# Handing out on-chip buffers by the engine that read them last, and two reorderings, in a four-layer WKV and graph-convolution kernel

## The chip, the cores and the metric

The kernel runs on one core of a Trainium2 chip. Its time is the device time of one launch in microseconds (us), the median over runs. Five engines matter, and each works through its own list of instructions in order. PE (TensorE) multiplies matrices. DVE (VectorE) does the recurrences, the weighted sums and the products. ACT (ScalarE) does exponentials, logarithms and squares. POOL (GpSimd) does further elementwise work, and SP (SyncE) issues the DMA transfers. An instruction waits on a semaphore when another engine must have finished first. While it waits, everything behind it on its own engine waits too.

## The reference

The input `x` is 16 x 192 x 56 x 56 in float32, so there are 16 samples with 192 channels and 3136 positions each. Four layers follow one another, each as `x = x + layer(group_norm(x))`. Three layers are bidirectional WKV layers, and the fourth is a graph convolution with a batch norm and a GELU. Cut to what matters:

```python
def wkv_layer(x):                            # x is already group-normed
    xs = x.reshape(B, C, T).transpose(0, 2, 1)
    k, v, r = xs @ Wk.T, xs @ Wv.T, xs @ Wr.T
    x_bi = 0.5 * (wkv_scan(k, v) + flip(wkv_scan(flip(k), flip(v))))
    h = sigmoid(r) * x_bi
    h = layer_norm(h) * ln_g + ln_b          # over the channels
    return h @ Wo.T

# wkv_scan keeps two decayed sums along the positions:
#   p = decay * p + exp(k) * v,   q = decay * q + exp(k)
#   y = (p_before + exp(u + k) * v) / (q_before + exp(u + k))

def graph_layer(x):                          # x is already group-normed
    m = max(roll(x, 2, H) - x, roll(x, -2, H) - x, roll(x, 2, W) - x, roll(x, -2, W) - x, 0)
    return gelu(batch_norm(conv1x1(concat(x, m))))
```

## The kernel before

**Tiling.** Two samples are worked on together as a pair, which gives eight pairs. The 2 x 192 channels fill three blocks of 128 partitions. The positions are cut into seven chunks of `L = 448`. One tile holds one chunk of a pair: 128 partitions x 3 blocks x 448 positions, and a few columns at the edges for the carry of a scan. Such a tile is a *slot*; there are 33 (`NSLOTS`), and nearly all large data of the kernel lives in them: a chunk of `x`, the keys `ek = exp(k)`, the values `ekv = exp(k) * v`, the two scans' outputs `q` and `p`, the gate `sg`, and scratch for the graph layer. `class Slot` takes the slot that has been free for longest from the list `free`, and `give` puts one back at its end. A slot is given back in program order, when its last reader has been written into the program; whoever takes it next waits on a semaphore until that reader has really finished.

**Steps.** Two pairs are under way at a time, half a layer apart. Of one, the forward part is worked on (the functions `a_...`: keys, values, the scans `q` and `p` from left to right, and `y = p / q`). Of the other it is the backward part (`b_...`: the scans from right to left, the mix of both directions with the gate, the layer norm, the output product and its addition to `x`). One step does one chunk of each. The order of all instructions within a step is written out by hand in one function for each kind of step, and the program keeps that order on every engine. Mapped onto the trace, there are 85 steps `both_a`, 17 `both_a_first` (the first chunk of a layer's forward part), 42 `both_c` (a backward chunk beside a chunk of the graph layer), 66 `forward_a`, and 39 others.

**The functions that the change touches.** `scan` (line 870) takes a slot for its output and issues three scans on DVE, one for each block. `bonus` (line 885) issues two DVE instructions, one over two blocks and one over one; `a_den`, `a_num`, `b_den` and `b_num` call it. `a_p` is the forward scan `p`, followed by `save` (line 881), which copies its last column into the edge of the next chunk's `ekv`. `a_y` (line 977) is one POOL product over the whole tile. `b_mix` (lines 1026 to 1028) is nine POOL products and sums; at its end it gives back the slot of `ekv`, called `y` there, and that of `sg`. `b_sums` (lines 1042 and 1044) has PE add up squares for the layer norm. `b_rs1`, `b_rs2`, `b_rs3` (1050, 1058, 1060) make its deviation on ACT. `b_spread` (1066) spreads it over partitions on PE into `rsb`, `b_scale` (1071) multiplies by it on DVE, `b_out` is the output product on PE into `ops`, and `b_x` (1084) adds that to `x` on DVE. Of the group norm of a pair's next layer, `norm_var` (744 to 760) makes the variance on DVE from PE's result `psg` and two ACT instructions `rstd` (752, 753). `norm_fold` (772 to 775) refines it on DVE and folds it into the weights on ACT. The parts of these norms stand in one list, and each call of `gap()` takes the next part off it and issues it there. `c_rows` (1109 to 1111) and `c_columns` (1120 to 1124) are the neighbour maxima of the graph layer on DVE, and `c_product` its matrix product on PE.

Of the kernel before, what the change touches and what calls it, by code (L numbers as in the profile page):

```python
# [58 lines left out]
NSLOTS = 33  # L59
# [414 lines left out]
def fast_path(ctx: ExitStack, tc: tile.TileContext, flag, x, wproj, wfold, wcfold, wconst, wgroup, sums, picks, vecs, out):  # L474
# [22 lines left out]
        return f"{s}_{ngen[0]}"  # L497


    free = [f"slot{i}" for i in range(NSLOTS)]  # L500

    class Slot:
        def __init__(self, what):
            self.tag = free.pop(0)
            rows = keep.tile([P, 3, L + 4], F32, tag=self.tag, name=name(what))
            self.full, self.lead = rows[:, :, 2 : L + 3], rows[:, :, 1 : L + 2]
            self.t = rows[:, :, 2 : L + 2]

        def give(self):
            free.append(self.tag)  # L510


    free_banks = [f"bank{i}" for i in range(7)]
# [303 lines left out]
    def gap(eng=V):  # L817
        if norms:
            part, run = norms.pop(0)
            if part is norm_fold:  # L820
                part(run, eng)
            else:
                part(run)
# [35 lines left out]
    def scan(run, key, data, step, first):  # L859

        dec = params[run.l][0]
        s = Slot(key)
        for j in ORDER:
            if first:
                out, e = s.t[:, j, ::step], data.t[:, j, ::step]
            elif step > 0:
                out, e = s.lead[:, j, :], data.lead[:, j, :]
            else:
                out, e = s.full[:, j, ::-1], data.full[:, j, ::-1]
            V.tensor_tensor_scan(  # L870
                out, dec[:, column(j)].to_broadcast([P, L if first else L + 1]), e, 0.0, ALU.mult, ALU.add
            )
        return s

    def save(s, step, to, eng=G):

        src, dst = (s.t[:, :, L - 1 : L], to.lead[:, :, 0:1]) if step > 0 else (s.t[:, :, 0:1], to.full[:, :, L : L + 1])
        if eng is S:
            S.activation(dst, src, AF.Copy)  # L879
        else:  # L880
            eng.tensor_copy(dst, src)  # L881
# [5 lines left out]

    AHEAD, BACK = 1, -1

    def slot_of(slots, c, what):  # L890
        if c not in slots:
            slots[c] = Slot(what)
        return slots[c]


# [6 lines left out]
    def a_keys(run, c):  # L902
        if not once(run, "k", c):
            return
        product(run, "k", run.w[0], run.xa[c], c == 0)
        slot_of(run.ek, c, "ek")
        if c == 0:
            take_bias(run, "k", S)

# [41 lines left out]
    def a_p(run, c, eng=G):  # L951
        run.h[c] = scan(run, "p", run.ekv[c], AHEAD, c == 0)
        if c < NL - 1:
            save(run.h[c], AHEAD, slot_of(run.ekv, c + 1, "ekv"), eng)

    def a_den(run, c):
        if c in (0, NL - 1):
# [8 lines left out]
    def a_num(run, c):  # L966
        bonus(run, run.h[c], run.ekv[c], run.h[c])

    def ln(s, js=slice(0, 3)):
        S.activation(s.t[:, js, :], s.t[:, js, :], AF.Ln)  # L970

    def exp_minus(s, js=slice(0, 3)):
        S.activation(s.t[:, js, :], s.t[:, js, :], AF.Exp, scale=-1.0)  # L973

    def a_y(run, c):
        den = run.den.pop(c)
        G.tensor_mul(run.h[c].t, run.h[c].t, den.t)  # L977
        den.give()


    def b_gate(run, c):
# [25 lines left out]
    def b_den(run, c):  # L1007
        q = run.q.pop(c)
        bonus(run, run.ek[c], run.ek[c], q)
        q.give()  # L1010

    def b_p(run, c):
        if c not in run.p:
# [4 lines left out]
    def b_num(run, c):  # L1018
        p = run.p.pop(c)
        bonus(run, run.ekv[c], run.ekv[c], p)  # L1020
        p.give()

    def b_mix(run, c):
        y, h, sg, den = run.ekv.pop(c), run.h[c], run.sg.pop(c), run.ek[c]
        for j in ORDER:
            G.tensor_mul(y.t[:, j, :], y.t[:, j, :], den.t[:, j, :])  # L1026
            G.tensor_add(h.t[:, j, :], h.t[:, j, :], y.t[:, j, :])  # L1027
            G.tensor_mul(h.t[:, j, :], h.t[:, j, :], sg.t[:, j, :])  # L1028
        y.give()
        sg.give()  # L1030

    def b_squares(run, c, js=ORDER):
        h, sq = run.h[c].t, run.ek[c].t
# [3 lines left out]
    def b_sums(run, c):  # L1037
        h, sq = run.h[c].t, run.ek.pop(c)
        st = run.ps["st"] = bank("st")
        parts = ((h, 0), (h, 1), (sq.t, 0), (sq.t, 1))  # L1040
        for n, (t, i) in enumerate(parts):
            PE.matmul(st[32 * n : 32 * n + 32, :L], ones[:, 0, :], t[:, 2 * i, :], start=True, stop=False)
        for n, (t, i) in enumerate(parts):
            PE.matmul(st[32 * n : 32 * n + 32, :L], ones[:, 1 + i, :], t[:, 1, :], start=False, stop=n < 2)  # L1044
        sq.give()

    def b_rs1(run, c):
        rs, st = row.tile([P, L], F32, tag="rs", name=name("rs")), run.ps["st"]
# [25 lines left out]
    def b_out(run, c):  # L1074
        h = run.h.pop(c)
        run.ps["o"] = banks("ops")
        project(run.ps["o"], params[run.l][5], of(h.t), L)
        h.give()

    def b_x(run, c):  # L1080
        wob, ps, xs = params[run.l][4], run.ps["o"], run.xb[c]
# [31 lines left out]
    def c_columns(run, c):  # L1113

        m, xt, ml = run.m[c].t, run.xa[c].t, Slot("ml")
        run.ml[c] = ml
        for j in ORDER:
            xr = xt[:, j, :].rearrange("p (r w) -> p r w", w=W)
            mr = ml.t[:, j, :].rearrange("p (r w) -> p r w", w=W)
            V.tensor_max(mr[:, :, 2 : W - 2], xr[:, :, 0 : W - 4], xr[:, :, 4:W])  # L1120
            V.tensor_max(mr[:, :, 0:2], xr[:, :, W - 2 : W], xr[:, :, 2:4])
            V.tensor_max(mr[:, :, W - 2 : W], xr[:, :, W - 4 : W - 2], xr[:, :, 0:2])
        V.tensor_max(ml.t, ml.t, xt)  # L1123
        V.tensor_max(m, m, ml.t)
# [185 lines left out]
    def invert(t):  # L1310
        ln(t)
        exp_minus(t)
# [61 lines left out]
    def both_a_first(b, a, nback, nfront, loads):  # L1374

        den = lambda: a[0].den[a[1]]
        l = of_stage(0)
        load_ahead(nback)
        store()
        a_values(*a)  # L1380
        b_squares(*l, (0, 2))
        b_q(*b)
        b_sigmoid(*b)
        b_p(*b)
        b_den(*b)
        invert(b[0].ek[b[1]])
        b_num(*b)
        b_mix(*b)
        slot_of(a[0].ekv, a[1] + 1, "ekv")
        for u in loads:  # L1390
            load_ahead(u)
        a_ekv(*a)
        b_squares(*l, (1,))
        if nback is not None:
            b_gate(*nback[1:])
        b_sums(*l)
        b_rs1(*l)
        if nback is not None:
            b_exp(*nback[1:])
        a_q(*a)  # L1400
        b_rs2(*l)
        b_rs3(*l)
        keys(nfront)
        a_p(*a, V)
        spread_and_scale(l)
        b_squares(*b, (0,))
        a_save(*a)
        exp_keys(nfront)
        b_squares(*b, (2, 1))
        b_sums(*b)  # L1410
        a_den(*a)
        b_rs1(*b)
        ln(den())
        add(l)
        a_num(*a)
        late[b] = 0.5
        exp_minus(den())
        a_y(*a)

    def both_c(b, a, nback, nfront, loads):  # L1420

        l0, l1, l2 = of_stage(0), of_stage(1), of_stage(2)
        load_ahead(nback)
        first = nback is not None and not l1
        b_q(*b)
        b_p(*b)
        if first:

            b_gate(*nback[1:])
            b_exp(*nback[1:])  # L1430
            c_product(*a, 0)
        if l0:
            squares_and_sums(l0)
        b_den(*b)
        ln(b[0].ek[b[1]])
        if l0:
            b_rs1(*l0)
        exp_minus(b[0].ek[b[1]])
        if l2:
            add(l2)  # L1440
            sum_up()
        if l1:
            spread_and_scale(l1)
        gap()
        store()
        for u in loads:
            load_ahead(u)
        if nback is not None:
            if not first:
                b_gate(*nback[1:])  # L1450
                b_exp(*nback[1:])
        else:
            keys(nfront)
            exp_keys(nfront)
        if not first:
            c_product(*a, 0)
        c_rows(*a)
        if l0:
            b_rs2(*l0)
            b_rs3(*l0)  # L1460
            late[l0] = 1
        c_columns(*a)
        c_product(*a, 1)
        gap()
        gap()
        b_num(*b)
        b_sigmoid(*b)
        b_mix(*b)
        if l1:
            add(l1)  # L1470
            sum_up()
        if nback is not None:
            b_q(*nback[1:])
            b_p(*nback[1:])
        ahead = nback is None and l0 and nfront is not None and nfront[0] == "A"
        if ahead:
            a_q(*nfront[1:])
            a_save(*nfront[1:])
            b_spread(*l0)
            c_end(*a, False)  # L1480
            a_values(*nfront[1:])
            b_scale(*l0)
            b_out(*l0)
            late[l0] = 2
        elif l0:
            spread_and_scale(l0)
        if not ahead:
            c_end(*a, False)
        late[b] = 0
# [350 lines left out]
```

## Time and profile before

| what | value |
|---|---|
| median of 3 runs | 5248.44 us (5244.23 to 5249.13) |
| the profiled execution's own time | 5246.37 us |
| its span | 5244.4 us |
| DVE busy | 4837.0 us (92%), 6288 instructions |
| PE busy | 4701.2 us (90%), 15542 instructions |
| ACT busy | 3680.4 us (70%), 7163 instructions |
| POOL busy | 2900.0 us (55%), 2234 instructions |
| mean granted TensorE clock | 0.943 |
| DMA | 482.47 MB, mean 92 GB/s |

The profiled execution lies 2.1 us below the median. Its span is 2.0 us less than its own time, which is what lies around the program. "Busy" is time in which an engine had an instruction under way. The rest of an engine's span is idle, and the trace says which instruction of which engine ended each idle stretch. In the lines that follow, `p<-fdecays,ekv` is an instruction's output and its inputs by their names in the program, and `L870` is its line in the kernel. The number after the bar in a group's line is its busy time, then the mean of one instruction in ns, then the idle time just before these instructions with what ended most of it.

### The profile page before, as it was taken

Reading aid. Unit: us, or ns where it says so; the run is one execution under the profiler, and the core shown is the slowest. Engines: PE = TensorE matmul, PEld = TensorE weight load, DVE = VectorE, ACT = ScalarE, POOL = GpSimd, SP = SyncE. Lnnn points to the kernel's source line nnn. Section 1 sums busy time; section 2 is a strip of 40 time slices with the busy share of each in tenths; the row PEclk is TensorE's granted clock in tenths of the full one; section 3 lists DMA queues with packets and bytes.
Section 4 is the critical chain, followed back from the end, with each engine's and each line's share of the span. In section 5 each row is a group of like instructions: output and inputs, shape, how many; then the busy total and the mean of one; then the engine's idle time right before and its main releaser. Section 6 shows DMA issues by size and latency. Waiting matters only on the chain. (4 is left out here: it accounts for less than half of the span.)

```text
span 5244.4 us, 51899 instructions
## 1 busy us (share of the span) xinstructions
PE 4701.2 (90%) x15542; PEld 1493.0 (28%) x15542; DVE 4837.0 (92%) x6288; ACT 3680.4 (70%) x7163; POOL 2900.0 (55%) x2234
## 2 busy tenths in 40 slices
PE   7999998989899998898989999889898999999887
PEld 3222222223232222222323222222232322222222
DVE  6999889899999998999999999889999999999996
ACT  6777777776566777776656678778766667777672
POOL 1666555555455655555454556556545455666562
PEclk9999999999999999999999999999999999999998
DMA  5222222223232222223323223222332322222233
GB/s 153 69 82 82 95 82 92 85 90 116 89 116 71 87 90 88 85 85 100 118 79 113 84 74 100 87 78 93 115 100 87 111 74 76 75 83 81 73 108 114
DMA packets 314275, 482.47 MB, mean 92 GB/s; under 512 B 66432, under 2 KB 306688, under 8 KB 313984
## 3 DMA queue, kind: packets, MB, share of 16 engines
q1 hardware_dynamic: 312832, 477.59, 28.5%
q8 instruction: 125, 2.05, 0.2%
q10 hardware_dynamic: 1152, 1.48, 0.1%
q14 instruction: 166, 1.36, 0.1%
HBM read 324.83 MB, written 154.14 MB: 91 GB/s over the span
## 5 line engine op out<-in xcount | busy, mean ns | idle before, releaser
L870 DVE TENSOR_TENSOR_SCAN p<-fdecays,ekv 128x449 f32<-128x449 f32 (+1 forms) x1008 | 1021.9, 1069 | 113.8 <-POOL p L1027 60.1
L870 DVE TENSOR_TENSOR_SCAN q<-fdecays,ek 128x449 f32<-128x449 f32 (+1 forms) x1008 | 1024.7, 1072 | 8.9 <-ACT ek L915 8.8
L977 POOL TENSOR_TENSOR p<-p,q 128x1344 f32<-128x1344 f32 x168 | 511.6, 3045 | 838.2 <-ACT q L973 543.0
L1026 POOL TENSOR_TENSOR ekv<-ekv,ek 128x448 f32<-128x448 f32 x504 | 627.1, 1244 | 625.0 <-ACT ek L973 392.9
L1028 POOL TENSOR_TENSOR p<-p,sg 128x448 f32<-128x448 f32 x504 | 633.3, 1257 | 144.5 <-ACT ek L879 101.3
L1027 POOL TENSOR_TENSOR p<-p,ekv 128x448 f32<-128x448 f32 x504 | 600.9, 1192 | 39.5
L881 POOL COPY ekv<-p 128x3 f32<-128x3 f32 x265 | 221.8, 837 | 538.5 <-DVE p L870 531.5
L915 ACT ACTIVATE ek<-k,k 128x448 f32<-128x448 f32 x504 | 296.9, 633 | 213.1 <-PE k L596 168.1
L730 ACT ACTIVATE fjunk<-x 128x448 f32<-128x448 f32 x672 | 387.7, 577 | 39.4 <-DVE x L1084 13.0
L1035 ACT ACTIVATE ek<-p 128x448 f32<-128x448 f32 x504 | 279.4, 572 | 168.4 <-POOL p L1028 167.9
L1066 PE MATMUL rsb<-rs,fpicks 32*128 32x448 f32 (+1 forms) x1008 | 342.0, 602 | 46.8 <-ACT rs L1060 46.8
L991 ACT ACTIVATE sg<-r,r 128x448 f32<-128x448 f32 x504 | 313.1, 627 | 95.6 <-PE r L596 72.3
L885 DVE SCALAR_TENSOR_TENSOR ek<-ek,fcc,q 128x896 f32<-128x896 f32 x336 | 374.0, 1154 | 0.0
L1071 DVE TENSOR_TENSOR p<-p,rsb 128x448 f32<-128x448 f32 x504 | 281.7, 615 | 92.0 <-PE rsb L1066 92.0
L1084 DVE SCALAR_TENSOR_TENSOR x<-ops,fwob,x 128x448 f32<-128x448 f32 x504 | 315.6, 674 | 49.3 <-PE ops L596 30.2
L729 ACT ACTIVATE fjunk<-x 128x448 f32<-128x448 f32 x600 | 342.8, 571 | 11.4
L885 DVE SCALAR_TENSOR_TENSOR q<-ek,fcc,q 128x896 f32<-128x896 f32 x336 | 343.0, 1062 | 6.3 <-ACT cvb L949 4.6
L1050 ACT ACTIVATE rs<-st 64x448 f32<-64x448 f32 x168 | 90.2, 537 | 358.0 <-PE st L1044 358.0
L970 ACT ACTIVATE q<-q 128x1344 f32<-128x1344 f32 x168 | 221.7, 1319 | 162.1 <-DVE q L885 114.1
L593 PE MATMUL ops<-p,fwo 128*128 128x448 f32 x336 | 210.0, 713 | 139.6 <-DVE p L1071 139.3
L935 DVE SCALAR_TENSOR_TENSOR ekv<-v,v,ek 128x448 f32<-128x448 f32 x504 | 313.5, 676 | 11.9 <-PE v L602 5.7
L885 DVE SCALAR_TENSOR_TENSOR ekv<-ekv,fcc,p 128x896 f32<-128x896 f32 x336 | 322.2, 1000 | 0.0
(236 smaller groups left out, 11827.6 us busy)
## 6 DMA issues: line engine op xcount, KB each, us to landing
x<-xd SPq DMA_DIRECT2D x240, 672.0 KB, 5.2
xd<-x SPq DMA_DIRECT2D x168, 672.0 KB, 3.8
x<-in_x_dram SPq DMA_DIRECT2D x320, 224.0 KB, 4.1
x<-in_x_dram SPq DMA_DIRECT2D x320, 112.0 KB, 4.0
out_dram<-ml SPq DMA_DIRECT2D x112, 224.0 KB, 2.3
m<-xd SPq DMA_DIRECT2D x112, 168.0 KB, 4.8
wkv<-in_wfold_dram SPq DMA_DIRECT2D x24, 640.0 KB, 5.4
out_dram<-ml SPq DMA_DIRECT2D x112, 112.0 KB, 2.3
```

The lines of the kernel that those rows point to most:

```text
L729: S.activation(junk, xt[:, j, :], AF.Identity, accum_out=stats[:, 0, j, c : c + 1])
L730: S.activation(junk, xt[:, j, :], AF.Square, accum_out=stats[:, 1, j, c : c + 1])
L870: V.tensor_tensor_scan(out, dec[:, column(j)].to_broadcast([P, L if first else L + 1]), e, 0.0, ALU.mult, ALU.add)
L885: by_channel(lambda js, i: V.scalar_tensor_tensor(dst.t[:, js, :], e.t[:, js, :], cc[:, i : i + 1], state.t[:, js, :], ALU.mult, ALU.add))
L935: V.scalar_tensor_tensor(e.t[:, j, :], ps[j][:, 0:L], b[:, j, :], run.ek[c].t[:, j, :], ALU.add, ALU.mult)
L977: G.tensor_mul(run.h[c].t, run.h[c].t, den.t)
L991: S.activation(sg.t[:, j, :], ps[j][:, 0:L], AF.Exp, bias=b[:, j, :], scale=-1.0, accum_out=run.chk[:, at : at + 1])
L1026: G.tensor_mul(y.t[:, j, :], y.t[:, j, :], den.t[:, j, :])
L1027: G.tensor_add(h.t[:, j, :], h.t[:, j, :], y.t[:, j, :])
L1028: G.tensor_mul(h.t[:, j, :], h.t[:, j, :], sg.t[:, j, :])
L1066: PE.matmul(ps[j][:, :L], pick[rows, j, :], rs[rows, :], start=True, stop=True)
L1084: V.scalar_tensor_tensor(xj, ps[j][:, 0:L], wob[:, column(j)], xj, ALU.add, ALU.add, accum_out=run.new[:, 0, j, c : c + 1] if c == 0 else ...
```

## The change

There are three edits.

First, each free slot carries the engine that read it last, and a request may name an engine. The request then takes the slot that has been free longest among those of its own engine. If there is none, it takes the oldest slot whose last reader is not DVE (`V`), and otherwise the oldest of all. The scans ask for DVE's slots, the keys for PE's, and the slot that receives the edge of `p` for those of the engine that copies it. All other requests name no engine and so take the oldest slot not last read by DVE. Slots of `x`, of `m` and of `ml` are given back without an engine's name.

Second, in `both_a_first` the slot for the next chunk's `ekv` is no longer taken ahead of the scans. The copy of `p`'s edge goes from DVE to POOL (17 copies in the program). The order at the end of the step becomes both bonuses first and the addition to `x` behind them.

Third, in `both_c` one of the two calls of `gap()` behind the second graph product moves ahead of `c_columns`.

The order of the instructions on PE, ACT and SP stays the same. POOL's order gains only the 17 copies, each behind that step's `b_mix`. DVE loses them, and has in those 17 steps the two bonuses of `a_num` ahead of the three additions to `x`, and in seven `both_c` steps `norm_var` ahead of `c_columns`. What else changes is which slot each tile lies in, and so what each first writer of a slot waits for.

```diff
-    free = [f"slot{i}" for i in range(NSLOTS)]
+    free = [(f"slot{i}", None) for i in range(NSLOTS)]

     class Slot:
-        def __init__(self, what):
-            self.tag = free.pop(0)
+        def __init__(self, what, engine=None):
+            own = [slot for slot in free if engine is not None and slot[1] is engine]
+            slot = (own + [slot for slot in free if slot[1] is not V] + free)[0]
+            free.remove(slot)
+            self.tag = slot[0]
...
-        def give(self):
-            free.append(self.tag)
+        def give(self, engine=None):
+            free.append((self.tag, engine))
...
     def scan(run, key, data, step, first):
-        s = Slot(key)
+        s = Slot(key, V)
...
     def a_keys(run, c):
-        slot_of(run.ek, c, "ek")
+        slot_of(run.ek, c, "ek", PE)
...
     def a_p(run, c, eng=G):
         run.h[c] = scan(run, "p", run.ekv[c], AHEAD, c == 0)
         if c < NL - 1:
-            save(run.h[c], AHEAD, slot_of(run.ekv, c + 1, "ekv"), eng)
+            save(run.h[c], AHEAD, slot_of(run.ekv, c + 1, "ekv", eng), eng)
...
     a_y:    den.give()             ->  den.give(G)
     b_den:  q.give()               ->  q.give(V)
     b_num:  p.give()               ->  p.give(V)
     b_mix:  y.give(); sg.give()    ->  y.give(G); sg.give(G)
     b_sums: sq.give()              ->  sq.give(PE)
     b_out:  h.give()               ->  h.give(PE)
...
     def both_a_first(b, a, nback, nfront, loads):
         b_mix(*b)
-        slot_of(a[0].ekv, a[1] + 1, "ekv")
...
-        a_p(*a, V)
+        a_p(*a)
...
         b_rs1(*b)
-        ln(den())
-        add(l)
-        a_num(*a)
-        late[b] = 0.5
-        exp_minus(den())
+        late[b] = 0.5
+        invert(den())
+        a_num(*a)
+        add(l)
         a_y(*a)
...
     def both_c(b, a, nback, nfront, loads):
+        gap()
         c_columns(*a)
         c_product(*a, 1)
-        gap()
         gap()
```

More of the change, by code (lines that the diff above doesn't have):

```diff
@@ L888, in fast_path, with slot_of @@
     AHEAD, BACK = 1, -1
-    def slot_of(slots, c, what):
+    def slot_of(slots, c, what, engine=None):
         if c not in slots:
-            slots[c] = Slot(what)
+            slots[c] = Slot(what, engine)
         return slots[c]
@@ L977, in a_y @@
         G.tensor_mul(run.h[c].t, run.h[c].t, den.t)
-        den.give()
+        den.give(G)
     def b_gate(run, c):
@@ L1009, in b_den @@
         bonus(run, run.ek[c], run.ek[c], q)
-        q.give()
+        q.give(V)
     def b_p(run, c):
@@ L1020, in b_num @@
         bonus(run, run.ekv[c], run.ekv[c], p)
-        p.give()
+        p.give(V)
     def b_mix(run, c):
@@ L1028, in b_mix @@
             G.tensor_mul(h.t[:, j, :], h.t[:, j, :], sg.t[:, j, :])
-        y.give()
-        sg.give()
+        y.give(G)
+        sg.give(G)
     def b_squares(run, c, js=ORDER):
@@ L1044, in b_sums @@
             PE.matmul(st[32 * n : 32 * n + 32, :L], ones[:, 1 + i, :], t[:, 1, :], start=False, stop=n < 2)
-        sq.give()
+        sq.give(PE)
     def b_rs1(run, c):
@@ L1077, in b_out @@
         project(run.ps["o"], params[run.l][5], of(h.t), L)
-        h.give()
+        h.give(PE)
     def b_x(run, c):
```

## The prediction

> **What bounds the kernel now.** First the busy times of the page: which engine has the least idle time.
>
> ```profile
> PE 4701.2 (90%) x15542; PEld 1493.0 (28%) x15542; DVE 4837.0 (92%) x6288; ACT 3680.4 (70%) x7163; POOL 2900.0 (55%) x2234
> ```
>
> DVE is busy for 4837.0 of 5244.4 us. It idles for 407 us, so that is all that waits can give back. PE is close behind, but much of its time is matmuls stretched by waiting; the order in which the engines wait for each other decides. Second, DVE's waits by line and releaser (total us, times, longest):
>
> ```profile
> DVE p L1071 <- PE rsb L1066: 92.0, 54, 18.6
> DVE p L870 <- POOL p L1027: 60.1, 18, 6.8
> DVE p L870 <- POOL p L1028: 53.6, 6, 9.0
> DVE x L1084 <- PE ops L596: 30.2, 22, 4.4
> DVE gt L772 <- ACT rstd L753: 20.3, 8, 3.3
> ```
>
> The second and third lines are 24 waits and 113.8 us in which a `p` scan waits for the mix on POOL. No scan reads anything of the mix; it waits for the *slot* that the mix read last. Third, where they lie. This is DVE's timeline through one `both_a_first` (703.6 to 743.8 us, measured like every step below from the first backward scan to that of the next step), and POOL's:
>
> ```profile
> 718.21 3.04 DVE L870 TENSOR_TENSOR_SCAN q<-fdecays,ek 128x448 f32<-128x448 f32 x3
> 730.21 3.05 DVE L870 TENSOR_TENSOR_SCAN p<-fdecays,ekv 128x448 f32<-128x448 f32 x3 [8.95 <-POOL p L1028]
> 733.29 0.17 DVE L881 COPY ekv<-p 128x3 f32<-128x3 f32 x1
> 733.37 1.68 DVE L1071 TENSOR_TENSOR p<-p,rsb 128x448 f32<-128x448 f32 x3
> ...
> 739.22 1.28 DVE L1084 SCALAR_TENSOR_TENSOR x<-ops,fwob,x 128x448 f32<-128x448 f32 x2 [2.52 <-PE ops L596]
> 741.55 0.69 DVE L1084 SCALAR_TENSOR_TENSOR x<-ops,fwob,x 128x448 f32<-128x448 f32 x1 [1.05 <-PE ops L602]
> ```
> ```profile
> 729.04 1.13 POOL L1028 TENSOR_TENSOR p<-p,sg 128x448 f32<-128x448 f32 x1
> ```
>
> `scan p` could start at 721.25 and starts at 730.21, just after the mix's last instruction ends at 730.17. Behind it the scaling (L1071), the output product on PE and the addition to `x` are all late. A first step without such a wait, 333.9 to 365.6 us, has a different wait at the same place:
>
> ```profile
> 351.52 3.03 DVE L870 TENSOR_TENSOR_SCAN p<-fdecays,ekv 128x448 f32<-128x448 f32 x3
> ...
> 357.92 1.68 DVE L1071 TENSOR_TENSOR p<-p,rsb 128x448 f32<-128x448 f32 x3 [2.18 <-PE rsb L1066]
> ```
>
> So `rsb` is next in line, and `ops` came sooner there: DVE's two waits ahead of L1084 are 0.26 and 0.59 us.
>
> **Slots, in the first steps.** Six of the 17 first steps wait about 8.95 us and three about 6.8 us: 74 us. With the change the scan takes the oldest slot that DVE itself read last, that of a `q` or `p` just used by a bonus, so nothing of POOL is waited for. These nine steps last 37.72, 40.21, 39.85, 37.70, 40.25, 39.86, 37.72, 40.26 and 39.85 us, together 353.4. What comes next: in two other first steps with the same work (33.35 us each) no slot is waited for, `rsb` starts 24.6 us into the step as in the stalled ones, and DVE waits 3.8 us for it. I take 33.35 for all nine: 9 x 33.35 = 300.2, a gain of 53. The other 21 us become a wait of L1071 for `rsb`. Bounds: the whole 74, if `rsb` came earlier too, though nothing ahead of it on PE or ACT is moved, and 14, if the six longest only fall to the 37.7 us of the other three (6 x 2.3), for a cause that I do not see.
>
> Part of this gain is PE's speed. Behind the stall PE has been idle for 3.85 us, and its first two `ops` matmuls take 1.86 us; in the step at 333.9, where PE comes straight from `rsb`, the same pair takes 1.02. So DVE waits 3.57 us for `ops` in the stalled step and 0.26 + 0.59 in the other. The steps of 33.35 us have these short waits, so this is counted.
>
> **Slots, in `both_a`.** The other 15 waits, 2.2 to 2.9 us each, sum to 39.7. They lie in three kinds of stretches of five `both_a` steps in pairs 2 to 7, which last 126.6, 128.0 and 127.4 us, each kind three times. Without waits DVE alone would need 23.57 a step, as in the first pairs. But behind DVE stands a loop of ACT and POOL: from ACT's inversion of `q` (L970) to the mix 11.76 us, and from there to the end of `rs` (L1050) 12.8, so 24.56 a step. And bonuses that start earlier fall beside the mix. In this trace a pair of bonuses (L885) beside it took 3.32 us against 1.74 alone; a step like this without a slot wait took 25.97 instead of 24.68, 1.3 more. The Trainium skill (SBUF — State Buffer, Who interferes with whom) has a harsher rule: a DVE instruction with two inputs in SBUF and a GpSimd instruction that reads SBUF exclude each other for a whole instruction. A POOL instruction of the mix takes 1.14 us, so by the rule a bonus pair may lose 2 x 1.14 in each of the 15 steps, 34 of the 39.7 us. By the row it is 1.3, in the first step of a stretch. I take 25.97 + 4 x 24.56 = 124.2 for every stretch: gains of 2.4, 3.8 and 3.2, three times, 28 us. Bounds 39.7 - 34 = 6, and 40.
>
> **The order at the end of the first step.** Ahead of L1084 DVE waits 34.3 us in the 17 steps, but most of it lies in the stalled steps and goes with their stall, already counted. An unstalled step has 0.26 + 0.59 = 0.85, so 14.5 in all. With both bonuses ahead of the addition DVE is done about 1 us sooner. That is then waited for at the next step, whose L1071 already waits 0.92 for `rsb` at its start: ACT's `rs` hangs on PE's `st` behind the output product, and PE's order is unchanged. I take 0; bounds 0 and -14.5. The addition itself is up to 1.7 us later; the next use of that `x` is the store and the sums, a step later.
>
> **The copy of the edge.** 17 copies of 0.42 us leave DVE (7.2 us). In the same place DVE waits for `rsb`, so 0. On POOL a copy of that form takes 0.84 in the mean. It is queued behind `b_mix`; behind it are only `chk` and `a_y`, which starts much later since it needs both bonuses and the inversion. The copied edge is read by the next `p` scan, 20 us on: 0. If POOL had no such gap, it would be 17 x 0.84 = 14.
>
> **The group norm's parts.** Seven `both_c` steps have this, as here on DVE and ACT:
>
> ```profile
> 1210.83 3.45 DVE L1120 TENSOR_TENSOR ml<-x 128x416 f32<-128x416 f32 x1
> ...
> 1218.24 0.15 DVE L744 TENSOR_SCALAR nm<-psg 128x3 f32<-128x3 f32 x1
> ...
> 1222.57 0.16 DVE L772 TENSOR_TENSOR gt<-rstd 128x3 f32<-128x3 f32 x1 [3.31 <-ACT rstd L753]
> ```
> ```profile
> 1221.50 0.57 ACT L1060 ACTIVATE rs<-rs 64x448 f32<-64x448 f32 x1
> 1222.10 0.20 ACT L752 ACTIVATE rstd<-var 128x3 f32<-128x3 f32 x1
> ```
>
> `rstd` is late because ACT is, and its input was ready at 1219. Moving `norm_var` up cannot bring it forward. And `psg` comes from PE at about 1216.3, while `c_rows` ends at 1209.2: DVE now waits 7.1 us there, and `c_columns`, 9.0 us long, is queued behind that wait. Later it no longer meets the mix (L1120 took 3.45 beside it, 1.53 otherwise), so it takes about 5.9, and `norm_fold` starts near 1216.3 + 0.9 + 5.9 = 1223.1 instead of 1222.57. I take +0.7 x 7 = +5. Bounds: -20 (the wait goes and nothing comes), and +15 if `c_product`, 5 us later on PE, delays `rsb`, which is needed at 1230.8.
>
> **Sum.** -53 - 28 + 5 = -76 on the profiled 5246.4, so 5170. The median lies 2.1 us above: 5172.
>
> **Rivals.** *All waits come back* (0.12): 113.8 + 34.3 + 20.3 + 7.2 = 176 us, 5073. For it: DVE has the least idle time. Against it: `rsb`, seen as the next wait.
>
> *The next waits take more* (0.22): bonuses and the ACT and POOL loop take back all of `both_a`'s gain, and the norm costs 5: 5248.4 - 53 + 5 = 5200.
>
> *The slots arrive late elsewhere* (0.07), slower. A key's slot is now the one that PE reads last in the output product. Its first writer is ACT's edge copy L879, and behind that on ACT the exponentials of the keys are queued, which release PE's banks. In a `both_a` step that copy starts at 405.99 and the output product ends at 404.8, a margin of 1.2 us. If PE were 2.1 us later in each step, ACT would wait 0.9 us in each of 85 steps, which is the 76 gained: that is the turning point. At 2.3 us it is 1.1 x 85 = 94, and the time 5248.4 - 76 + 94 = 5266. Against it: PE is 2 us late only in the steps behind a stall.
>
> *The slots do not come out as meant* (0.03): where DVE has none of its own, a scan takes the oldest other one, perhaps POOL's, and the waits stay: 5246.
>
> **How the numbers follow.** The likeliest case has 0.56, and its own range is about 5140 to 5195. The range from 5112 to 5213 takes in the second rival with some room. It leaves out the first rival except its near edge, the slower one and the empty one, together about 2 in 10. This kernel's runs can tell 0.2% (10.5 us) from no change. Faster by more: 0.56 + 0.12 + 0.22 = 0.90, less 0.01 for the far end of the second. Within: 0.04. Slower: 0.07.
>
> **What would show it.** Right: no `p` scan waiting for POOL L1027 or L1028; first steps of about 33.4 us with a wait of L1071 for `rsb` of about 3.8; DVE's total for L1071 up from 92 to about 115; a wait of L744 for `psg` of 7 us in seven steps; `both_a` stretches near 124. Wrong: ACT's L879 waiting for PE `ops`, DVE scans waiting for ACT or DMA, or first steps still above 37.

## The result, and the profile after

The changed kernel takes 5235.34 us (median of 17 runs, 5231.05 to 5239.18) against 5247.15 us before (17 runs). The ratio is 0.9978, with a 95% interval from 0.9971 to 0.9986. That is 0.2% faster, or 12 us, where 76 us were forecast. The waits that the change was to remove are gone, and most of the gain was lost again elsewhere. Of the profile after, first the busy times and DVE's waits (line numbers are higher by 5 than before):

```profile
PE 4730.8 (90%) x15542; PEld 1497.6 (29%) x15542; DVE 4844.9 (93%) x6271; ACT 3680.5 (70%) x7163; POOL 2911.8 (56%) x2251
```
```profile
DVE p L1076 <- PE rsb L1071: 182.7, 84, 21.0
DVE nm L749 <- PE psg L607: 51.0, 12, 8.5
DVE mv L740 <- ACT fjunk L735: 22.6, 12, 16.3
DVE x L1089 <- PE ops L601: 11.7, 7, 4.0
```

No `p` scan waits for POOL any more (113.8 us before), and the waits for `ops` have shrunk from 48.6 to 20.5 us. But the wait of the scaling for `rsb` has gone from 92.0 us in 54 waits to 182.7 us in 84, far past the 115 forecast. The first step that was shown before lasts 32.2 us now instead of 40.2. This is DVE's timeline in it:

```profile
716.01 3.04 DVE L875 TENSOR_TENSOR_SCAN q<-fdecays,ek 128x448 f32<-128x448 f32 x3
718.97 3.02 DVE L875 TENSOR_TENSOR_SCAN p<-fdecays,ekv 128x448 f32<-128x448 f32 x3
726.19 1.68 DVE L1076 TENSOR_TENSOR p<-p,rsb 128x448 f32<-128x448 f32 x3 [4.20 <-PE rsb L1071]
...
731.11 1.86 DVE L1089 SCALAR_TENSOR_TENSOR x<-ops,fwob,x 128x448 f32<-128x448 f32 x3
```

The scan follows at once, the scaling waits 4.20 us for `rsb`, and the addition behind the bonuses waits for nothing. All this is as forecast. Summed over kinds of steps in the two profiled executions, which are 10.7 us apart (a step goes from its first scan on DVE to that of the next):

| steps | before | after | difference |
|---|---|---|---|
| 17 `both_a_first` | 605.0 | 523.4 | -81.6 |
| 45 `both_a` with statistics of `x` (nine stretches of five) | 1146.0 | 1181.4 | +35.4 |
| 40 other `both_a` | 952.2 | 960.2 | +8.0 |
| all else, with the program's start | 2541.1 | 2568.7 | +27.6 |

So the loss lies in the 45 `both_a` steps above all: they were to fall by 28 us and rose by 35. (Beside their own chunks, they sum up the inputs of pairs 2 to 7; the prediction calls them stretches "in pairs 2 to 7", but the chunks that they work on are those of pairs 0 to 5, counted from 0.) In 17 of them a step lasts 27.1 to 27.3 us; these are called the locked steps below. One of them, at 594.84 to 622.16, on DVE:

```profile
602.45 1.74 DVE L890 SCALAR_TENSOR_TENSOR ekv<-ekv,fcc,p 128x896 f32<-128x896 f32 x2
606.75 1.69 DVE L1076 TENSOR_TENSOR p<-p,rsb 128x448 f32<-128x448 f32 x3 [2.57 <-PE rsb L1071]
...
617.82 2.59 DVE L890 SCALAR_TENSOR_TENSOR q<-ek,fcc,q 128x896 f32<-128x896 f32 x2
```

POOL, PE and ACT in the same step, each from its own timeline:

```profile
608.37 1.15 POOL L1031 TENSOR_TENSOR ekv<-ekv,ek 128x448 f32<-128x448 f32 x1 [6.39 <-ACT ek L978]
...
616.68 1.15 POOL L1032 TENSOR_TENSOR p<-p,ekv 128x448 f32<-128x448 f32 x1
617.90 2.03 POOL L1033 TENSOR_TENSOR p<-p,sg 128x448 f32<-128x448 f32 x1
```
```profile
619.99 0.95 PE L1049 MATMUL st<-p,fsums 128*32 128x448 f32 x4 [2.09 <-POOL p L1033]
620.60 1.40 PE L1049 MATMUL st<-ek,fsums 128*32 128x448 f32 x4
621.92 1.86 PE L598 MATMUL r<-x,wr 128*128 128x448 f32 x2
```
```profile
622.03 0.54 ACT L1055 ACTIVATE rs<-st 64x448 f32<-64x448 f32 x1 [1.49 <-PE st L1049]
622.47 1.31 ACT L975 ACTIVATE q<-q 128x1344 f32<-128x1344 f32 x1
623.82 1.33 ACT L978 ACTIVATE q<-q 128x1344 f32<-128x1344 f32 x1
625.87 0.64 ACT L996 ACTIVATE sg<-r,r 128x448 f32<-128x448 f32 x1 [0.73 <-PE r L601]
```

Read as a round, which is what has to happen between one start of `rs` and the next: ACT's `rs` is followed on ACT by the inversions, the gate and `ek`. Then POOL mixes (608.37), ACT squares, PE sums, and at 622.03 the next `rs` begins. The one before began at 594.69, so a round takes 27.34 us, and the step lasts as long. DVE only follows. Two things in the round are slower than they need be. The last instruction of the mix takes 2.03 us instead of 1.14, beside a bonus on DVE that takes 2.59. And PE, which waited 2.09 us for that mix, then takes 1.86 us for a pair of `r` matmuls that elsewhere takes 1.02, so that ACT waits for `r`.

### The profile page after: what moved, and what is told of

Same layout as the page of the kernel before. It is cut to its first block, busy times and chain, and to the rows that moved or that the text cites. A ratio compares the mean times of both kernels' runs of the same rounds, so it can differ in the third digit from the quotient of the medians.

```text
span 5233.7 us, 51955 instructions
## 1 busy us (share of the span) xinstructions
PE 4730.8 (90%) x15542; PEld 1497.6 (29%) x15542; DVE 4844.9 (93%) x6271; ACT 3680.5 (70%) x7163; POOL 2911.8 (56%) x2251
## 3 DMA queue, kind: packets, MB, share of 16 engines
q10 hardware_dynamic: 1152, 1.48, 0.1%
## 5 line engine op out<-in xcount | busy, mean ns | idle before, releaser
L1033 POOL TENSOR_TENSOR p<-p,sg 128x448 f32<-128x448 f32 x504 | 652.0, 1294 | 144.5 <-ACT ek L884 100.1
L1076 DVE TENSOR_TENSOR p<-p,rsb 128x448 f32<-128x448 f32 x504 | 281.9, 612 | 183.4 <-PE rsb L1071 182.7
L890 DVE SCALAR_TENSOR_TENSOR ek<-ek,fcc,q 128x896 f32<-128x896 f32 x336 | 391.0, 1203 | 0.0
L890 DVE SCALAR_TENSOR_TENSOR q<-ek,fcc,q 128x896 f32<-128x896 f32 x336 | 358.9, 1107 | 6.3 <-ACT cvb L954 4.7
L890 DVE SCALAR_TENSOR_TENSOR p<-ekv,fcc,p 128x896 f32<-128x896 f32 x336 | 296.1, 921 | 6.4 <-POOL ekv L886 1.7
```

The lines of the kernel that those rows point to most:

```text
L890: by_channel(lambda js, i: V.scalar_tensor_tensor(dst.t[:, js, :], e.t[:, js, :], cc[:, i : i + 1], state.t[:, js, :], ALU.mult, ALU.add))
```

## Experiments

Three theories were held against each other: (A) the slots' gain is taken back by this round, (B) by the norm's parts, (C) by the order in the first step. The first five kernels do parts of the change.

**The slots alone** (e_slots: the first edit; `both_a_first` and `both_c` as before).

> Only the first edit: slots by their last reader; the order of the first step and of the group norm's parts as before. Theory A (the loop): the gain of the slots is taken back in the both_a steps that also make statistics of x, where ACT, POOL and PE now wait for each other in a loop that is longer than DVE's work. Then this kernel shows both at once: the first steps some 60 us shorter, the both_a stretches of pairs 2 to 7 some 25 us longer, about -20 to -35 us in all. Theory B (the norm's parts): the slots bring what was forecast, about -80 us, and the loss comes from the third edit. Theory C (the order of the first step): about -60 us, and the loss comes from the second edit.

Measured: 5266.61 us against 5243.82, ratio 1.0051 (1.0037 to 1.0065), so 0.5% *slower*. The 45 `both_a` steps are 29.3 us longer, as theory A has it. But the first steps lost only 15.6 us, not 60: six of them still last 40.0 to 40.5 us. ACT's timeline in one of these:

```profile
729.28 0.64 ACT L996 ACTIVATE sg<-r,r 128x448 f32<-128x448 f32 x1 [6.21 <-POOL p L1032]
```

The scan no longer waits for the mix, but the gate does: it got a slot that the mix reads, and `rs` and `rsb` are queued behind it. The wait has moved from DVE to ACT.

**The first step's order alone** (e_first: the second edit).

> Only the second edit: in the first step of a layer the edge copy on POOL, its slot taken later, and the addition to x behind both bonuses; slots from the oldest, norm's parts as before. Theory A: little of its own, 0 to -15 us, since each first step ends about 1 us sooner and the next step waits that much longer for rsb; the slot waits of p for POOL stay. Theory B: 0. Theory C: +20 to +40 us.

Measured: 5224.23 us, ratio 0.9964 (0.9950 to 0.9978), a gain of 20 us, more than any theory said, and at least as much as the whole change gains. The first steps fall by 55 us. No scan waits for L1028 any more, presumably since a slot taken later comes from another place of the list, and the rest waits for the mix's earlier instruction:

```profile
DVE p L870 <- POOL p L1027: 79.7, 21, 6.9
```

**The norm's part alone, and the change without it** (e_gap and e_nogap: the third edit).

```diff
     both_c:
+        gap()
         c_columns(*a)
         c_product(*a, 1)
-        gap()
         gap()
```

> Only the third edit: norm_var ahead of c_columns. Theory A: 0 to +10 us; the wait for rstd (20 us) goes and a wait for psg (about 50 us) comes, but c_columns behind it is shorter. Theory B: +30 us or more. Theory C: 0.

> The changed kernel without the third edit. Theory A: within 8 us of the changed kernel, which is 12 us below the one before. Theory B: 30 us or more below the changed kernel. Theory C: within 8 us of the changed kernel.

Measured: alone 5234.74 us, ratio 0.9985 (0.9978 to 0.9991), a small gain where none was expected; half of its 21 runs lie near 5231 us and half near 5241, so its size is uncertain. The change without it: 5230.15 us, ratio 0.9976 (0.9968 to 0.9983), not to be told from the whole change (0.9978). So theory B falls. In the trace of the edit alone, 5.1 us shorter than that of the kernel before, the first steps lose 12.3 us, though the edit does not touch them, and other steps gain; why is open.

**The slots alone, with the first step's slot taken later** (e_late).

```diff
     both_a_first of the kernel with the slots alone:
         b_mix(*b)
-        slot_of(a[0].ekv, a[1] + 1, "ekv")
```

> As e_slots (only the first edit), but the first step's slot for the next ekv is taken behind the scan p instead of ahead of it; the edge copy stays on DVE. In e_slots the wait of the scan for POOL (9 us) had moved to ACT, whose gate sg got a slot that the mix read. If taking the slot early is what leaves the gate that one, the six steps of 40.5 us fall to about 33.3: 40 to 50 us below e_slots, near 5220. If the gate gets such a slot anyway, it stays within 8 us of e_slots.

Measured: 5234.43 us, ratio 0.9981 (0.9973 to 0.9989), 32 us below the slots alone. The six steps fall from 40.5 to between 31.6 and 33.2 us, and all 17 together by 50, so the early slot was what left the gate the wrong one. The whole gains less than that, since other steps give 18 us back, 6 of them the 45 `both_a` steps. DVE's waits show where the wait went last:

```profile
DVE ekv L886 <- POOL p L1032: 21.1, 6, 3.9
```

That is the edge copy on DVE, and it costs little, since the scaling behind it would wait for `rsb` anyway. In the whole change POOL does this copy.

**The round, shortened** (e_count). The other seven kernels ask what sets the 27.3 us.

```diff
     both_a:
-        count(z)
         b_q(*b)
...
         a_save(*a)
-        count(z)
+        count(z, 2)
```

> The changed kernel, with the first of a both_a step's two pieces of statistics of x (two ACT squarings with their readouts, 1.4 us) moved from ACT's chain between rs and the mix to behind the edge copy of q, where ACT has to wait for the mix anyway. No work is added or left out. Theory A (the loop ACT, POOL, ACT, PE sets these steps at 27.3 us, DVE does not): the locked steps get at least 1.4 us shorter, and more if PE then no longer idles and slows down: -25 to -50 us against the changed kernel (ratio 0.988 to 0.993 to the one before). Rival D (the longer steps come from DVE and POOL excluding each other, wherever ACT stands): within 8 us of the changed kernel (0.998).

Measured: 5149.73 us against 5244.38, ratio 0.9819 (0.9806 to 0.9833). The changed kernel's ratio of 0.9978 puts it at 5233 us in this comparison, so the move gains 83 us, more than expected, with the same work. The 45 `both_a` steps last 1094.3 us instead of 1181.4, and the locked ones now last 23.6 to 24.2. DVE sets the pace again, as here:

```profile
603.21 1.68 DVE L1076 TENSOR_TENSOR p<-p,rsb 128x448 f32<-128x448 f32 x3 [0.25 <-PE rsb L1071]
...
614.27 1.72 DVE L890 SCALAR_TENSOR_TENSOR q<-ek,fcc,q 128x896 f32<-128x896 f32 x2
```

The bonus takes 1.72 us, clear of the mix. Rival D, in which only that overlap counts, expected no gain from moving ACT's work; but since the move also ends the overlap, the next run is needed to weigh the two.

**More work on DVE** (e_delay), a block of a scan done twice:

```diff
     scan:
-        for j in ORDER:
+        for j in ORDER + ((1,) if again else ()):
...
     both_a:
+        busy = len(z) > 0
...
-        a_p(*a)
+        a_p(*a, G, busy)
```

> The changed kernel with work added: in both_a steps with statistics of x, the forward scan p does its last block twice, 1.0 us more on DVE, with the same result. Decays come from PSUM, so it has one input in SBUF. It pushes DVE's bonus past the end of the mix. Rival D (DVE's bonus, by excluding POOL's last mix instruction, lengthens it from 1.14 to 2.03 us, and that is what makes the loop longer): the locked steps get 0.9 us shorter, -5 to -15 us in all against the changed kernel. Theory A without a part for this exclusion: the locked steps stay at 27.3, since DVE waits 2.6 us for rsb there and hides the 1.0; +5 to +20 us from the other steps.

Measured: 5179.64 us, ratio 0.9878 (0.9863 to 0.9893). With a scan of 1.02 us *added* in 48 steps (these 45, and three others with some statistics) the kernel is 53 us faster than the changed one, far outside what either theory expected. DVE and PE in a step of it:

```profile
613.72 4.17 DVE L875 TENSOR_TENSOR_SCAN p<-fdecays,ekv 128x449 f32<-128x449 f32 x4
617.81 1.72 DVE L890 SCALAR_TENSOR_TENSOR q<-ek,fcc,q 128x896 f32<-128x896 f32 x2
```
```profile
617.96 0.94 PE L1049 MATMUL st<-p,fsums 128*32 128x448 f32 x4 [1.20 <-POOL p L1033]
618.57 0.95 PE L1049 MATMUL st<-ek,fsums 128*32 128x448 f32 x4
619.45 1.02 PE L598 MATMUL r<-x,wr 128*128 128x448 f32 x2
```

The bonus starts as the mix ends, and both take their usual time. PE waits 1.20 us instead of 2.09, and its `r` pair takes 1.02 us again instead of 1.86. The locked steps last 24.79 us, near DVE's own 23.57 with the added scan. So the overlap stands at the start of the chain: without it a step is 2.5 us shorter, though POOL itself loses only 0.9 by it.

**More work on PE** (e_warm), five matmuls into a bank that the sums then overwrite:

```diff
     b_sums:
+        for _ in range(warm):
+            PE.matmul(st[:, :L], params[run.l][5](0, 0), h[:, 0, :], start=True, stop=True)
...
     both_a:
-        b_sums(*b)
+        b_sums(*b, 5 if busy else 0)
```

> The changed kernel with work added: in both_a steps with statistics of x, PE does five more matmuls of 128x448 into the bank of st just ahead of the first sums, which overwrite them, about 2.1 us. They fill the time in which PE waits for the mix's last part. Theory A with its second half (PE idles 2.1 us behind the first sums, its granted clock falls, the r product that follows takes 1.7 us longer and ACT waits 1.3 us for it in each round of the loop): the locked steps fall from 27.3 to about 25.5 us though PE has more to do, -20 to -35 us against the changed kernel. Without the second half (the slow product is only a consequence): 0 to +30 us.

Measured: 5269.69 us, ratio 1.0050 (1.0036 to 1.0063), slower. The locked steps fell to 26.41 us. But the `forward_a` step behind each stretch grew by about 4 us, 47 in all. ACT's copy `cvb` is queued there behind `rs`, which waits for the sums, and these came late. DVE's waits have it, with 34.2 us where the changed kernel has 4.7:

```profile
DVE q L890 <- ACT cvb L954: 34.2, 17, 3.4
```

The same with the moved statistics:

> Both the moved statistics and the added matmuls. Theory A with both halves: the locked steps fall to 24 to 24.5 us, where DVE's own work (23.6 us) sets them; -45 to -60 us against the changed kernel. If the moved statistics alone already keep PE from idling, the matmuls bring nothing or cost up to 2 us a step.

Measured: 5270.27 us, ratio 1.0050 (1.0037 to 1.0064). The locked steps last 26.41 us here too, with ACT's work moved or not, which points to the five matmuls themselves being in the way. With three, and none in a layer's last step (e_warm2, `3 if busy and b[1] > 0 else 0`):

> As e_warm, with three added matmuls instead of five, and none in the last both_a step of a layer, where the five delayed ACT's copy behind them and cost some 4 us in each of twelve forward steps. Theory A with its second half: the locked steps fall to 26.0 to 26.4 us, -12 to -25 us against the changed kernel. Without it: 0 to +20 us.

Measured: 5205.17 us against 5242.18, ratio 0.9919 (0.9905 to 0.9933). The changed kernel's 0.9978 would be 5231 us here, so this is 26 us faster (31 by the ratios), with more work on PE. The locked steps last 25.70 us. ACT's and PE's timelines in one:

```profile
619.98 0.95 PE L1051 MATMUL st<-ek,fsums 128*32 128x448 f32 x4
620.86 1.02 PE L598 MATMUL r<-x,wr 128*128 128x448 f32 x2
```
```profile
620.98 0.54 ACT L1057 ACTIVATE rs<-st 64x448 f32<-64x448 f32 x1 [1.05 <-PE st L1051]
625.48 0.64 ACT L996 ACTIVATE sg<-r,r 128x448 f32<-128x448 f32 x1 [0.17 <-PE r L607]
```

POOL's last mix instruction still takes 2.04 us here, so of the 27.3 us some 1.6 came from PE's slow matmuls alone, and the other 0.9 of the 2.5 from the overlap itself. The changed kernel's own trace agrees: in one round of it PE's matmuls were not slowed, and with the overlap there (2.01 us for the last mix instruction) it takes 25.68 us, like the locked steps here:

```profile
3406.34 0.54 ACT L1055 ACTIVATE rs<-st 64x448 f32<-64x448 f32 x1 [1.05 <-PE st L1049]
3432.02 0.54 ACT L1055 ACTIVATE rs<-st 64x448 f32<-64x448 f32 x1 [1.05 <-PE st L1049]
```

**The moved statistics without the change, and with the change but for the third edit.**

> The kernel before, with the same move of one piece of statistics as in e_count, and nothing of the change. Theory A (the change's slots bring what was forecast once the loop no longer sets these steps): the waits of p for POOL stay here, so -5 to -30 us against the kernel before; the changed kernel with the move then lies 65 to 90 us below this one, near the forecast 76. Rival E (the move alone is worth its 83 us, whatever the slots): -70 to -90 us against the kernel before, and the change on top is worth the same 12 us as without the move.

> The changed kernel with the moved statistics, and without the third edit. With the loop out of the way the norm's parts may show their own price: 0 to -10 us against e_count if the wait for psg costs, as forecast (+5 us for the edit); 0 to +10 us if the wait for rstd that comes back costs more.

Measured: without the change 5213.35 us, ratio 0.9943 (0.9930 to 0.9957); with it, but without the third edit, 5146.21 us, ratio 0.9809 (0.9795 to 0.9822). So the move is worth 0.6% to the kernel before and about 1.6% to the changed one. The other way round, the change is worth 0.2% without the move and 1.2% with it: 0.9819 / 0.9943 = 0.9875, some 65 us, near the forecast 76. That is the lower end of what theory A expected (65 to 90), and far from rival E's 12. That it comes so near the forecast is in part luck: between the two traces the first steps fall by 75.8 us (53 were forecast), the 45 `both_a` by 14.3 (28 were), and other steps give 26 back. The third edit makes no difference that these runs tell. The last kernel, the change without its third edit and with the moved statistics, has the lowest time of all here, though e_count is not to be told from it.

## Why the prediction was wrong

The forecast was 76 us and the two traces differ by 10.7. Of the missing 65 us, 63 lie in the 45 `both_a` steps. Other steps lost some 31 us more than forecast, and the first steps gained 29 more.

**The bound.** Right that DVE was waiting for POOL's slots and not for data. The prediction named the round of ACT and POOL behind it, but took its size wrongly.

**Slots, in the first steps (-53).** Right in kind, and put too small. The nine stalled steps fell from 353.4 to 283.0 us. The whole group lost 81.6, of which some 13 came back in the `both_a` steps right behind: 14 of the 17 grew, by 0.65 to 1.04 us. The prediction did not see that the slots alone would have moved the wait to ACT's gate: alone they take 15.6 us off the first steps (e_slots), with the later taking of one slot 66 (e_late), and the second edit without them 55 (e_first). The later taking, which it treated only as part of the copy's move, is what most of this gain needs.

**Slots, in `both_a` (-28).** This is the step that failed. The stretches were put at 124.2 us and last 129.6 to 132.8. The period of the round was taken as 11.76 (inversion to mix) + 12.8 (mix to the end of `rs`) = 24.56, and is 27.34. In the round shown above the two parts measure 13.24 and 14.20 (and the next inversion starts 0.10 before `rs` ends). Of the 1.48 in the first part, 0.75 and 0.53 are ACT's waits for `r`, the rest small gaps. Of the 1.4 in the second, 0.89 is the mix's last instruction, 2.03 instead of 1.14, and 0.46 PE's second group of sums, 1.40 instead of 0.94. The prediction did price the overlap of bonus and mix, but as a loss of DVE, which had time to spare; it is POOL's loss that lies in the round.

And the two parts fit the step at 577.62 (11.77 and 12.82), in which a stall had just held DVE up. The trace before shows both cases. Here is PE behind that stall (first two lines), and in a step of 25.97 us without a slot wait, at 743.81 (the other two):

```profile
598.43 0.95 PE L1044 MATMUL st<-p,fsums 128*32 128x448 f32 x4 [0.96 <-POOL p L1028]
599.91 1.02 PE L593 MATMUL r<-x,wr 128*128 128x448 f32 x2
767.27 0.89 PE L1044 MATMUL st<-p,fsums 128*32 128x448 f32 x2 [2.08 <-POOL p L1028]
769.52 1.64 PE L593 MATMUL r<-x,wr 128*128 128x448 f32 x2
```

Behind the stall PE idled for 0.96 us and its `r` pair took 1.02. In the other step it idled for 2.08, and the pair took 1.64. There the round, from mix to mix, took 27.06 us already, which the prediction overlooked:

```profile
755.66 1.14 POOL L1026 TENSOR_TENSOR ekv<-ekv,ek 128x448 f32<-128x448 f32 x1 [4.76 <-ACT ek L973]
...
782.72 1.15 POOL L1026 TENSOR_TENSOR ekv<-ekv,ek 128x448 f32<-128x448 f32 x1 [5.79 <-ACT ek L973]
```

So the waits for the slots had kept DVE's bonus off the mix (behind the stall the mix ended at 598.38 and the bonus began at 600.18), much as the added scan does.

**Order at the end of the first step (0).** Right: an unstalled first step ends about 1.2 us sooner (31.75 to 30.53), and the following one lasts 1.0 longer (24.69 to 25.71).

**The copy of the edge (0).** Right in size: e_late, with the copy left on DVE, puts its wait of up to 3.9 us where the scaling would have waited.

**The norm's parts (+5).** Right in mechanism: the wait for `psg` of 7.07 us came, for `rstd` almost none is left, and the norm's refinement begins just as `c_columns` ends. The runs do not show a cost of the edit as a whole. Of the 27.6 us that the rest lost, where 5 were forecast, 11.2 lie in six of the graph-layer steps with no backward part, and without this edit they lose nothing; 10.0 lie in the `both_c` steps, and 7.6 of them come without this edit too; 5.7 lie in the steps with a backward part alone, and the slots alone lose as much there. The causes of these small parts stay open.

**The rivals.** "The next waits take more" (5200) had the right kind of cause and too small a size. "The slots arrive late elsewhere" came true only for the slots alone, on ACT's gate instead of the keys. The signs named for a wrong forecast did not show in the changed kernel. What showed is that two signs of a right one failed: the total for `rsb`, 182.7 us instead of 115, and the stretches, 131 us in the mean instead of 124.

## What to carry to other kernels

When a wait is removed from the engine that looks like the bound, add up the next round *from start to start*, with every wait that it has when nothing holds the others up. Rows taken behind a stall are too kind to it. A pause that looks like pure loss may be keeping two engines from colliding: if adding work on the waiting engine makes the kernel faster, shorten the round that it waits for. Buffers handed out by their last reader move a wait rather than remove it, until it is known who gets the slot that is left; here the second edit alone, with the old rule, gained at least as much as the whole change.

## What was unexpected in the hardware

PE's granted clock fell to half after a short idleness, but not each time. Two stretches of the changed kernel (length, busy times of PE, its weight loads, DVE, ACT and POOL, then the granted clock), and PE's idleness at the start of the second:

```profile
620.95:624.36 3.41, 3.41 (x8) 1.18 (x4) 3.41 (x5) 2.30 (x3) 0.00 (x0) 0.50 0.26 48
3430.00:3436.00 6.00, 4.94 (x18) 1.45 (x18) 5.92 (x7) 4.49 (x7) 1.63 (x3) 1.00 0.55 169
```
```profile
3430.42 0.95 PE L1049 MATMUL st<-p,fsums 128*32 128x448 f32 x4 [2.09 <-POOL p L1033]
```

In the round shown above PE was idle for 2.09 us up to 619.99, and from 620.95 the granted clock was 0.50 for 3.41 us, in which the slow `r` pair lies. At 3430.42 PE had been idle just as long, and the clock stayed at 1.00. In the changed kernel's 48 steps with statistics PE idles for 2.1 to 2.4 us at this place 35 times; the clock fell behind 29 of these and not behind 6. In e_delay it idles for 1.2 to 1.5 us there 36 times, and the clock never fell. The Trainium skill (TensorE: Matmul & The Clock Gate, Part 1: The HAM clock gate) sets about 3.4 us of idleness for this. Here less did it in most rounds and failed to in some, so the idle time alone is not the measure. What PE did just before, narrow sums of 32 columns, may count too, but no run here separates that.

On the exclusion between DVE and GpSimd the skill (SBUF — State Buffer, Who interferes with whom) agrees with the rows: both sides lose about 0.9 us where a bonus meets the mix, 2.59 against 1.72 and 2.03 against 1.14. They seem to take turns: in the round shown, the first of the two bonus instructions takes its usual 1.12 us, POOL's ends 0.99 after it, and the second, 1.55 instead of 0.68, ends 0.48 after POOL's. Which of the two engines lies on the round decides what the meeting costs.
